# The first layer of a graph network on one core: one ScalarE sum for the ranks of two edge tiles, widened blocks for both halves, one set of rows per group

## The chip, the cores and the metric

The kernel runs on one core of a Trainium2 chip. The time is device time of one execution in microseconds (us), and the median over runs is compared. The engines go by their short names: PE multiplies matrices (PEld is its loading of weights), DVE is VectorE, ACT is ScalarE, POOL is GpSimd, and SP is SyncE, which here issues most DMAs. Each engine works off its own list of instructions in order and waits on semaphores for the others.

## What is computed

There are N = 12500 nodes with 256 features and E = 200000 edges, sorted by their target `dst`. Two layers follow each other. The change touches the first one only:

```python
# L0: x (N,256) -> 4 heads of 32 columns, for "self" (order 0) and "neighbour" (order 1)
feat = relu(einsum('nd,ohdk->ohnk', x, W) + b)
att_s = leaky(einsum('hnk,hk->hn', feat[0], a_self))
att_n = leaky(einsum('hnk,hk->hn', feat[1], a_neigh))
edge_w = (att_s[:, src] + att_n[:, dst]) * edge_weight
agg = segment_sum(edge_w[..., None] * feat[1][:, dst, :], src, N)     # by src, which is not sorted
feat = stack([feat[0], agg]); feat = normalised over each head, scaled, shifted
x = layernorm(x + concat(feat))
# L1: messages relu([x[src], x[dst]] @ W_msg + b_msg), summed by dst; update, two layernorms
```

## The kernel before

The program has three stages on one time axis.

**Stage one** (`with ExitStack() as l0`) cuts the edges into 112 groups (`NG`) of 14 tiles (`GT`) of 128 edges. Since `dst` is sorted, a group's targets lie in a window of 128 rows of x, whose first row is read into a register (`base_reg`). For each group two things are made.

- *Features* (`feat_tasks`): `load_group` fetches the window's rows `xw` for the neighbour half and, for the first 98 groups (`NB` blocks of 128 rows), also the aligned row block `xb` for the self half. `transposes` and `keep` turn both, `project` multiplies them with the weights, `relu`, `att_mult`, `att_sum`, `mean_sum` and `centre` make centred features `F` and attention scores. `part0` to `part3` split the neighbour half into three bf16 parts `F3`. The self half goes to DRAM (`out_f`, to `selfd`), its scores stay in SBUF (`atts`, by `leaky_s`).
- *A counting sort by source block* (`sort_tasks`): the 14 tiles' edges are put in order of their source's block of 128 nodes. `widen` (ACT) spreads the block numbers of the first seven tiles over 99 columns. `hot` compares these with a ramp, `hot_b` compares the other seven tiles' block numbers, broadcast, with the ramp; both make the one-hots `A`. `pair`, `ranks`, `quarter`, `rows`, `begins`, `keep_v` give, for each edge's partition and each block, the rank `V` at which an edge of that block goes. `place_mm` (PE) puts `V + BIG * A` in PSUM for each tile, in chunks of 5, 5 and 4 tiles. `place_pick` (ACT, 14 times a group) takes relu of that minus `BIG` and sums it over the columns: one rank for each edge of a tile. `split` (DVE) splits the ranks in row and column numbers, `hot_r`, `goods`, `hot_q` (DVE) and `permute` (PE) move the edges' data to their places, `rel_keep`, `rel_turn`, `rel_row`, `rel_out`, `rel_in` bring the target rows over DRAM to all partitions, and `hot_n` makes one-hots `oT` of them. `message` (PE) multiplies these with `F3`, `evict` (ACT) copies the products to SBUF, and four `scatter`s (POOL, indirect DMAs) write them to a log in DRAM, in which each source block has its own stretch. `extras` writes the edges' source and weight beside the messages.

Every eighth group a chunk of edge data (`meta_load`, `meta_tasks`: names `m_...`) is prepared for the next eight.

The order is written out by hand: the table `AT` gives each task of group g a place `256 * g + AT[name]`, and all tasks of all groups are sorted by it. PE, ACT, DVE and SP each issue their tasks in that order (`manual_schedule`, which names these four engines and not POOL). A place modulo 256 tells what lies beside what: 256 units are one group.

**Stage two** (`with ExitStack() as bar`) goes through the 98 source blocks: `log_load` fetches a block's log, `log_hot` and `log_sum` sum it with one-hot matmuls, `heads_a` to `heads_d` combine the two sums with the self scores and normalise, `own_s` to `own_d` do the same for the self half `fs`, which `load_y` fetches from `selfd`, and `stats` to `store_x1` make the rows for layer two. **Stage three** (`with ExitStack() as l1`) goes through the edges again, 14 tiles a group, gathers source rows (L1346) and sums messages.

Of the kernel before, what the change touches and what calls it, by code (L numbers as in the profile page):

```python
# [11 lines left out]
def _warn_once_fixed(msg, *args, **kwargs):  # L12
# [28 lines left out]
    "widen": -453, "hot": -365, "hot_b": -265, "pair": -179, "ranks": -86, "quarter": -64, "rows": -29,  # L41
    "begins": 13, "keep_begins": 55, "keep_v": 51, "shift": 161, "reach": 262, "steps": 227, "steps_keep": 243,
    "steps_low": 256, "target": 313, "index": 400, "place_mm0": 52, "place_mm1": 63, "place_mm2": 204,
    "pick0": 73, "pick1": 78, "pick2": 78, "pick3": 87, "pick4": 123, "pick5": 144, "pick6": 156, "pick7": 170,
    "pick8": 179, "pick9": 219, "pick10": 229, "pick11": 239, "pick12": 249, "pick13": 280, "split": 339,
    "hot_r": 358, "goods": 374, "hot_q": 371, "permute": 424, "rel_keep": 435, "extras": 477, "rel_turn": 502,
    "rel_row": 552, "rel_out": 574, "rel_in": 595, "hot_n": 959, "message0": 997, "evict0": 1053,
    "message1": 1032, "evict1": 1063, "message2": 1056, "evict2": 1082, "message3": 1065, "evict3": 1121,
    "message4": 1101, "evict4": 1165, "message5": 1188, "evict5": 1203, "scatter0": 1120, "scatter1": 1146,
    "scatter2": 1197, "scatter3": 1206, "load": -331, "transposes": 47, "keep": 68, "project": 80, "relu": 295,  # L50
    "att_mult": 355, "mean_sum": 459, "att_sum": 438, "centre": 467, "leaky_n": 498, "part0": 584, "part1": 636,
    "part2": 665, "part3": 705, "leaky_s": 585, "out_f": 634, "m_load": -1689, "m_cast0": -1234,
    "m_cast1": -1433, "m_col0": -1201, "m_keep0": -1125, "m_col1": -698, "m_keep1": -614, "m_col2": -941,
    "m_keep2": -861, "m_block": -1073, "m_place": -877, "m_high": -378, "m_rest": -285, "m_mid": 263,
    "m_low": 351, "m_win": -76, "m_turn": -866, "m_pairs": -710, "m_mask": -535, "m_count": 210,
}
BIG = 4096.0
# [43 lines left out]
def kernel(  # L101
# [45 lines left out]
    selfd = dram.tile([ROWS, HD], FT, name="selfd")  # L147
# [12 lines left out]
    atts = consts.tile([P, NB, H], FT, name="atts")  # L160
# [55 lines left out]
    with ExitStack() as l0:  # L216
# [28 lines left out]
        nc.vector.memset(nbig, -BIG)  # L245
        quart = dcp.tile([P, 1], FT, name="quart")
# [178 lines left out]
        xb = {}  # L425
        F3 = {}

        def load_group(g):
            if g < NG:
                b = base_reg(g) if g else 0  # L430
                xw[g] = xin.tile([P, D], FT, name="xw")
                nc.sync.dma_start(xw[g], x[bass.ds(b, P), :])
            if g < NB:
                xb[g] = xin.tile([P, D], FT, name="xb")
                n = min(P, N - g * P)
                if n < P:
                    nc.vector.memset(xb[g], 0.0)
                nc.sync.dma_start(xb[g][:n], x[g * P:g * P + n, :])

        def feat_tasks(g):  # L440

            ww, bb = g < NG, g < NB
            o0, o1 = (0 if bb else 1), (2 if ww else 1)
            lo, hi = o0 * HD, o1 * HD
            st = {}

            def flat(t):
                return t[:, lo:hi]

            def heads(t):  # L450
                return t[:, lo:hi].rearrange("p (a k) -> p a k", k=32)

            def transposes():
                tp = ps.tile([P, 512], FT, name="tp", bufs=1)
                if ww:
                    for c in range(2):
                        nc.tensor.transpose(tp[:, c * P:(c + 1) * P], xw[g][:, c * P:(c + 1) * P], ident)
                if bb:
                    for c in range(2):
                        nc.tensor.transpose(tp[:, (2 + c) * P:(3 + c) * P], xb[g][:, c * P:(c + 1) * P], ident)  # L460
                st["tp"] = tp

            def keep():
                xT = feat.tile([P, 4, P], FT, name="xT")
                a, z = (0 if ww else 2), (4 if bb else 2)
                nc.scalar.copy(xT[:, a:z].rearrange("p c q -> p (c q)"), st["tp"][:, a * P:z * P])
                st["xT"] = xT

            def project():
                fp = bank[g][:, 0:D] if ww else ps.tile([P, 512], FT, name="fs")[:, 0:D]  # L470
                nc.tensor.matmul(fp[:, lo:hi], ones3, bias3[:, lo:hi], start=True, stop=False)
                for o in range(o0, o1):
                    for c in range(2):
                        nc.tensor.matmul(
                            fp[:, o * HD:(o + 1) * HD], st["xT"][:, (2 + c) if o == 0 else c, :],
                            w0s[:, c, o * 4:(o + 1) * 4, :].rearrange("p a k -> p (a k)"),
                            start=False, stop=(o == o1 - 1 and c == 1))
                st["fp"] = fp
# [69 lines left out]
        def sort_tasks(g):  # L548
# [97 lines left out]
            def place_pick(t):  # L646
                def f():
                    i, k = divmod(t, 5)
                    if t == 0:
                        small("sl", GT, p=P)  # L650
# [1040 lines left out]
```

## Time and profile before

| what | value |
|---|---|
| median of 10 runs | 4406.07 us (4403.0 to 4410.87) |
| profiled execution: time, span | 4406.86 us, 4405.1 us |
| stage one: first scatter starts, last scatter starts | 53.5 us, 1079.1 us |
| stage two: first and last matmul of L972 start | 1088.6 us, 1999.6 us |
| stage three: first and last matmul of L1424 start | 2027.3 us, 4390.0 us |
| granted PE clock, whole span | 0.924 |

The span is what the profiled instructions cover; the time of that execution is 1.8 us longer and lies within the ten runs. The page cuts the span in 40 slices of 110 us and gives the busy share of each in tenths, 9 for 90% or more:

```profile
PE   8999999997999999997777777777777777777776
...
DVE  9999999996999999995545555555555555555555
ACT  8999999996122222224444444444444444444444
POOL 2555555555666666664666666666666666666664
PEclk9999999998999999998888889889889898888888
```

The first ten slices are stage one, the next eight stage two, the rest stage three. In other views a line reads: source line, engine, operation, output<-inputs by the program's names, shapes; then either count, busy time, mean duration and idle time before, or (in a timeline) start and duration first. Where the engine stood idle before an instruction, a timeline line ends with the idle time and what ended it in brackets.

### The profile page before, as it was taken

Reading aid. Unit: us, or ns where it says so; the run is one execution under the profiler, and the core shown is the slowest. Engines: PE = TensorE matmul, PEld = TensorE weight load, DVE = VectorE, ACT = ScalarE, POOL = GpSimd, SP = SyncE. Lnnn points to the kernel's source line nnn. Section 1 sums busy time; section 2 is a strip of 40 time slices with the busy share of each in tenths; the row PEclk is TensorE's granted clock in tenths of the full one; section 3 lists DMA queues with packets and bytes.
Section 4 is the critical chain, followed back from the end, with each engine's and each line's share of the span. In section 5 each row is a group of like instructions: output and inputs, shape, how many; then the busy total and the mean of one; then the engine's idle time right before and its main releaser. Section 6 shows DMA issues by size and latency. Waiting matters only on the chain. (4 is left out here: it accounts for less than half of the span.)

```text
span 4405.1 us, 82564 instructions
## 1 busy us (share of the span) xinstructions
PE 3701.0 (84%) x24976; PEld 3130.7 (71%) x24976; DVE 3164.1 (72%) x9205; ACT 2374.0 (54%) x8379; POOL 2667.8 (61%) x2542
## 2 busy tenths in 40 slices
PE   8999999997999999997777777777777777777776
PEld 6888888876888888885666666656665666666665
DVE  9999999996999999995545555555555555555555
ACT  8999999996122222224444444444444444444444
POOL 2555555555666666664666666666666666666664
PEclk9999999998999999998888889889889898888888
DMA  5887766666666666664555555555555555555554
GB/s 193 278 270 264 247 216 217 218 202 212 180 192 191 190 192 190 192 187 127 145 144 144 140 145 143 140 143 143 146 139 146 140 144 144 147 141 142 141 144 113
DMA packets 470159, 763.55 MB, mean 173 GB/s; under 512 B 76202, under 2 KB 313504, under 8 KB 469712
## 3 DMA queue, kind: packets, MB, share of 16 engines
q1 hardware_dynamic: 339552, 415.13, 33.2%
q0 software_dynamic: 110848, 327.87, 24.2%
q10 hardware_dynamic: 19312, 15.21, 1.1%
q8 instruction: 204, 3.34, 0.3%
q14 instruction: 243, 1.99, 0.2%
HBM read 559.81 MB, written 198.12 MB: 172 GB/s over the span
## 5 line engine op out<-in xcount | busy, mean ns | idle before, releaser
L1346 POOL DMA_INDIRECT gb<-pd,srcf x1563 | 1501.7, 961 | 881.5 <-issue 483.2
L1424 PE MATMUL agg<-gb,o 128*128 128x256 f32 x3126 | 940.4, 429 | 309.7 <-ACT gb L1407 183.5
L1405 DVE TENSOR_TENSOR gb<-qp,gb 128x512 f32<-128x512 f32 x781 | 531.7, 681 | 768.7 <-remote 206.2
L1424 PEld LDWEIGHTS agg<-gb,o 128*128 128x128 f32 x3126 | 645.6, 215 | 485.6 <-ACT gb L1407 233.0
L731 POOL DMA_INDIRECT log<-m,ix x448 | 550.6, 1229 | 527.3 <-ACT m L725 148.3
L972 PE MATMUL sum<-lg,o 128*128 128x256 f32 x3724 | 839.3, 379 | 15.3 <-DMA lg<-log 13.7
L1407 ACT ACTIVATE gb<-gb 128x512 f32<-128x512 f32 x781 | 486.7, 626 | 645.6 <-DVE gb L1405 443.8
L972 PEld LDWEIGHTS sum<-lg,o 128*128 128x128 f32 x3724 | 696.0, 189 | 115.8 <-POOL lg L959 13.8
L964 DVE TENSOR_SCALAR o<-iotap,lg 128x128 f32<-128x128 f32 x1862 | 612.9, 399 | 38.9 <-PE sum L972 31.0
L651 ACT ACTIVATE junk<-wp,nbig 128x99 bf16<-128x99 f32 x1568 | 602.2, 457 | 1.2 <-PE wp L624 0.7
L1383 PE MATMUL qp<-qh,oT 128*128 128x256 f32 x1563 | 596.9, 401 | 4.4 <-DVE rs L1253 1.6
L959 POOL TENSOR_TENSOR lg<-lg 128x512 f32<-128x512 f32 x392 | 431.7, 1114 | 224.8 <-DMA lg<-log 161.8
L651 ACT ACTIVATION_READ_ACCUMULATOR junk<-wp,nbig 128x1 f32 x1568 | 472.2, 314 | 0.0
L1383 PE MATMUL qp<-ql,oT 128*128 128x256 f32 x1563 | 440.7, 301 | 0.0
L718 PE MATMUL mp<-F,oT 128*128 128x132 bf16 x5376 | 418.2, 222 | 21.7 <-ACT m L725 8.5
L718 PEld LDWEIGHTS <-oT 128*128 128x128 bf16 x5376 | 343.3, 99 | 53.5 <-issue 19.2
L1391 ACT ACTIVATE o<-iotac,rel 128x128 f32<-128x128 f32 x782 | 267.8, 391 | 180.0 <-PE agg L1424 76.1
L725 ACT COPY m<-mp 128x396 f32<-128x396 f32 (+1 forms) x672 | 349.7, 565 | 16.2 <-PE mp L718 11.0
L1383 PEld LDWEIGHTS qp<-qh,oT 128*128 128x128 f32 x1563 | 331.5, 212 | 31.7 <-PE agg L1424 4.3
L1383 PEld LDWEIGHTS qp<-ql,oT 128*128 128x128 f32 x1563 | 331.0, 212 | 24.6
L1387 DVE TENSOR_TENSOR o<-iotac,rel 128x256 f32<-128x256 f32 x390 | 161.3, 414 | 241.5 <-remote 55.7
L890 PE MATMUL qm<-wms,xT 128*128 128x256 f32 x224 | 97.9, 527 | 273.0 <-ACT xT L885 193.6
(263 smaller groups left out, 6566.3 us busy)
## 6 DMA issues: line engine op xcount, KB each, us to landing
lg<-log SPq DMA_DIRECT2D x392, 268.0 KB
dr<-in_dst_dram SPq DMA_DIRECT2D x781, 128.0 KB
rr<-reld SPq DMA_DIRECT2D x112, 512.0 KB
log<-zero SPq DMA_DIRECT2D x101, 268.0 KB
gb<-pd,srcf POOLq DMA_INDIRECT x1563
lg<-log SPq DMA_DIRECT2D x98, 201.0 KB
xw<-in_x_dram SPq DMA_DIRECT2D x112, 128.0 KB
xw<-x1d SPq DMA_DIRECT2D x112, 128.0 KB
```

Of the source, the lines that this page charges most:

```text
L651: nc.scalar.activation(small("junk", NBX, BF, p=P), st["w", i][:, k * NBE:k * NBE + NBX], AF.Relu, bias=nbig, accum_out=st["sl"][:, t:t + 1])
L718: nc.tensor.matmul(mp[:, r * (HD + H):(r + 1) * (HD + H)], st["oT"][:, r0 + r], F3[g][:, k], start=(k == 0), stop=(k == 2))
L725: nc.scalar.copy(st["m"][:, r0:r0 + n, 0:HD + H], st.pop(("mp", i))[:, :n * (HD + H)].rearrange("p (r w) -> p r w", r=n))
L731: ins = nc.gpsimd.indirect_dma_start(out=log[:, :], out_offset=bass.IndirectOffsetOnAxis(ap=st["ix"][:, k:k + 1], axis=0), in_=st["m"][:, ...
L959: e.tensor_tensor(t[:, 1, :n, 0:HD].rearrange("p r (h k) -> p r h k", h=H), t[:, 0, :n, 0:HD].rearrange("p r (h k) -> p r h k", h=H), t[:, ...
L964: nc.vector.tensor_scalar(o[:, r], iotap, t[:, 0, r, MW - 2:MW - 1], t[:, 0, r, MW - 1:MW], op0=OP.is_equal, op1=OP.mult)
L972: nc.tensor.matmul(sums[b], o[:, r], t[:, :, r, 0:HD], start=(k == 0 and r == 0), stop=(k == NK - 1 and r == n - 1))
L1346: nc.gpsimd.indirect_dma_start(out=gb[s][:r, i], out_offset=None, in_=pd[:, :], in_offset=bass.IndirectOffsetOnAxis(ap=srci[:r, t:t + 1], ...
L1383: nc.tensor.matmul(qp[:r, i], oT[:, i * P:i * P + r], q, start=(k == 0), stop=(k == 1))
L1405: nc.vector.tensor_tensor(z, qp, z, op=OP.add)
L1407: nc.scalar.activation(z, z, AF.Relu)
L1424: nc.tensor.matmul(agg[g], o[:r, i], z[:r, i], start=(j == 0 and i == 0), stop=lastmm)
```

## The change

1. *Ranks of two tiles in one sum.* `BIG` becomes 2^23. `keep_w` (ACT) writes a second copy of `V` times `PACK` = 2048 beside it; `place_mm` uses `V` for even tiles and `2048 * V` for odd ones, in chunks of 4, 4, 4 and 2 tiles. `place_pick` runs seven times on two tiles' columns: the sum is the even tile's rank plus 2048 times the odd tile's. `unpack` (ACT) and `apart` (three small operations on POOL) take the two apart: the odd rank by rounding, the even one as the rest. `split` then reads the same 14 ranks as before.
2. *`widen` spreads all 14 tiles*, and `hot_b` compares widened blocks as `hot` does.
3. *Both halves of the features from the window's rows.* `xb` and its load, transposes and copies are gone; `project` makes 256 columns from `xw` in two matmuls. The self half is written to `selfd` at the window's rows, by a register's address, with the four self scores beside it (132 columns); windows overlap, and the rows that two of them share are written twice, with the same values. `atts` is gone: stage two reads the scores with `fs`, whose tile gets a third buffer. All 112 groups do the full work of both halves.
4. *`src_keep`*: the copy of the source column in `extras` goes from DVE to ACT.
5. *A new order*: nearly every entry of `AT` changes. The work put between named tasks at the start is kept in its order by `due`.

```diff
 AT = {
-    "widen": -453, "hot": -365, "hot_b": -265, "pair": -179, "ranks": -86, "quarter": -64, "rows": -29,
-    "begins": 13, "keep_begins": 55, "keep_v": 51, "shift": 161, "reach": 262, "steps": 227, "steps_keep": 243,
-    "steps_low": 256, "target": 313, "index": 400, "place_mm0": 52, "place_mm1": 63, "place_mm2": 204,
...
-    "rel_row": 552, "rel_out": 574, "rel_in": 595, "hot_n": 959, "message0": 997, "evict0": 1053,
...
-    "part2": 665, "part3": 705, "leaky_s": 585, "out_f": 634, "m_load": -1689, "m_cast0": -1234,
...
+    "widen": -485, "hot": -379, "hot_b": -361, "pair": -303, "ranks": -160, "quarter": -124, "rows": -119,
+    "begins": -64, "keep_begins": -22, "keep_v": -3, "shift": 31, "reach": 165, "steps": 131, "steps_keep": 205,
+    "steps_low": 259, "target": 261, "index": 333, "keep_w": -3, "place_mm0": 5, "place_mm1": 43,
+    "place_mm2": 64, "place_mm3": 165, "pick0": 43, "pick1": 50, "pick2": 111, "pick3": 147, "pick4": 149,
+    "pick5": 195, "pick6": 196, "unpack": 205, "apart": 281, "split": 290, "hot_r": 309, "goods": 359,
+    "hot_q": 357, "permute": 428, "rel_keep": 461, "extras": 529, "src_keep": 542, "rel_turn": 465,
+    "rel_row": 513, "rel_out": 555, "rel_in": 560, "hot_n": 818, "message0": 922, "evict0": 944,
...
+    "scatter2": 1124, "scatter3": 1153, "load": -402, "transposes": -250, "keep": -167, "project": 2,
+    "relu": 167, "att_mult": 184, "mean_sum": 517, "att_sum": 470, "centre": 546, "leaky_n": 607, "part0": 630,
+    "part1": 673, "part2": 741, "part3": 804, "leaky_s": 640, "out_f": 1160, "m_load": -1865, "m_cast0": -1677,
...
-BIG = 4096.0
+BIG = 2.0 ** 23
+PACK = 2048.0
...
-    selfd = dram.tile([ROWS, HD], FT, name="selfd")
+    selfd = dram.tile([ROWS, H + HD], FT, name="selfd")
...
         def load_group(g):
-            if g < NG:
-                b = base_reg(g) if g else 0
-                xw[g] = xin.tile([P, D], FT, name="xw")
-                nc.sync.dma_start(xw[g], x[bass.ds(b, P), :])
-            if g < NB:
-                xb[g] = xin.tile([P, D], FT, name="xb")
-                n = min(P, N - g * P)
-                if n < P:
-                    nc.vector.memset(xb[g], 0.0)
-                nc.sync.dma_start(xb[g][:n], x[g * P:g * P + n, :])
+            xreg[g] = base_reg(g) if g else 0
+            xw[g] = xin.tile([P, D], FT, name="xw")
+            nc.sync.dma_start(xw[g], x[bass.ds(xreg[g], P), :])
...
+                nc.tensor.matmul(fp, ones3, bias3, start=True, stop=False)
+                for c in range(2):
+                    nc.tensor.matmul(fp, st["xT"][:, c, :], w0s[:, c].rearrange("p a k -> p (a k)"),
+                                     start=False, stop=(c == 1))
...
             def out_f():
-                nc.sync.dma_start(selfd[g * P:(g + 1) * P, :], st["F"][:, 0:HD])
+                nc.sync.dma_start(selfd[bass.ds(xreg[g], P), :], st["F"][:, 0:H + HD])
...
-            CH = [(0, 5), (5, 5), (10, 4)]
+            CH = [(a, min(4, GT - a)) for a in range(0, GT, 4)]
...
             def widen():
-                st["bx"] = srt.tile([P, h, NBX], BF, name="bx")
-                nc.scalar.copy(st["bx"], blk[c][:, j * GT:j * GT + h, None].to_broadcast([P, h, NBX]))
+                st["bx"] = srt.tile([P, GT, NBX], BF, name="bx")
+                nc.scalar.copy(st["bx"], blk[c][:, tl, None].to_broadcast([P, GT, NBX]))
...
             def hot_b():
-                b = blk[c][:, j * GT + h:j * GT + GT, None].to_broadcast([P, h, NBX])
-                nc.vector.tensor_tensor(st["A"][:, h:], iotab[:, h:], b, op=OP.is_equal)
+                nc.vector.tensor_tensor(st["A"][:, h:], iotab[:, h:], st["bx"][:, h:], op=OP.is_equal)
...
             def keep_v():
-                nc.scalar.copy(small("v", NBE, FR, p=P), st["V"])
+                nc.scalar.copy(small("v", 2 * NBE, FR, p=P)[:, :NBE], st["V"])
+
+            def keep_w():
+                nc.scalar.activation(st["v"][:, NBE:], st["V"], AF.Copy, scale=PACK)
...
-                    nc.tensor.matmul(o, identr, st["v"][:, None, :].to_broadcast([P, n, NBE]),
+                    nc.tensor.matmul(wp[:, :n * NBE].rearrange("p (t b) -> p t b", b=2 * NBE), identr,
+                                     st["v"][:, None, :].to_broadcast([P, n // 2, 2 * NBE]),
                                      start=True, stop=False)
...
-                    nc.scalar.activation(small("junk", NBX, BF, p=P), st["w", i][:, k * NBE:k * NBE + NBX], AF.Relu,
-                                         bias=nbig, accum_out=st["sl"][:, t:t + 1])
+                    i, t = k // 2, 2 * k % 4
+                    if k == 0:
+                        small("s7", h, p=P)
+                    nc.scalar.activation(
+                        small("junk", 2 * NBX, BF, p=P).rearrange("p (t b) -> p t b", b=NBX),
+                        st["w", i][:, t * NBE:(t + 2) * NBE].rearrange("p (t b) -> p t b", b=NBE)[:, :, :NBX],
+                        AF.Relu, bias=nbig, accum_out=st["s7"][:, k:k + 1])
...
+            def unpack():
+                nc.scalar.activation(small("t7", h, p=P), st["s7"], AF.Identity, bias=nhalf, scale=1.0 / PACK)
+
+            def apart():
+                sl = small("sl", GT, p=P)
+                odd = sl.rearrange("p (k w) -> p k w", w=2)[:, :, 1]
+                nc.gpsimd.tensor_scalar(odd, st["t7"], MAGIC, -MAGIC, op0=OP.add, op1=OP.add)
+                even = sl.rearrange("p (k w) -> p k w", w=2)[:, :, 0]
+                nc.gpsimd.tensor_single_scalar(even, odd, PACK, op=OP.mult)
+                nc.gpsimd.tensor_tensor(even, st["s7"], even, op=OP.subtract)
...
             def extras():
                 m = st["m"] = msgp.tile([P, NR, MW], FT, name="m")
-                nc.vector.tensor_copy(m[:, :, MW - 2], st["go"][:, :, 1])
                 nc.vector.tensor_reduce(m[:, :, MW - 1], st["go"][:, :, 2:5], AX.X, OP.add)
+
+            def src_keep():
+                nc.scalar.copy(st["m"][:, :, MW - 2], st["go"][:, :, 1])
...
-        for g in range(max(NG, NB)):
+        for g in range(NG):
...
-                                    atts[:, b:b + n, :, None].to_broadcast([P, n, H, 32]), op=OP.mult)
+                                    fs.pop(q)[:, :n, 0:H, None].to_broadcast([P, n, H, 32]), op=OP.mult)
...
-            fs[q] = bw.tile([P, BB, HD], FT, name="fs")
+            f = fs[q] = bw.tile([P, BB, H + HD], FT, name="fs", bufs=3)
```

## The prediction

> **What bounds the kernel.** I read the busy time by stretches first, because the share of the span mixes three stages.
>
> ```profile
> core 0: us, PE busy (x) PEld busy (x) DVE busy (x) ACT busy (x) POOL busy (x), PEclk, DMA share, GB/s
> ...
> 300.00:500.00 200.00, 191.35 (x2343) 162.70 (x2342) 191.94 (x606) 196.86 (x980) 108.37 (x85) 0.99 0.79 266
> ...
> 1400.00:1600.00 200.00, 200.00 (x950) 174.10 (x949) 191.73 (x533) 47.33 (x111) 137.35 (x115) 1.00 0.65 189
> ```
>
> In the first stage (to about 1084 us) PE, DVE and ACT are all above 95%: nobody waits long, and no single share names the bound. The second stage (first sum matmul at 1088.6, last at 1999.6) is PE at 200.00 of 200, and the third (from 2027) runs the gathers; the change alters only operands there. So everything is decided by the pace of the 112 groups of stage one. The source view of the multiply of `goods`, once per group, gives that pace:
>
> ```profile
> L669 DVE TENSOR_TENSOR mv<-rh,em x85: 1310/1318/1323, 104.0 to 884.0; 128x1120 bf16<-128x1120 bf16 x85
> ...
> L669 DVE TENSOR_TENSOR mv<-rh,em x11: 1312/1318/1319, 958.1 to 1045.7; 128x1120 bf16<-128x1120 bf16 x11
> ```
>
> 84 steps in 780.0 us are 9.29 us per group; the last groups, which have no second row block, take 87.6/10 = 8.76.
>
> Which engine sets 9.29? The durations of neighbours overlap, so I take from the timeline, for every shape, the median time from its start to the next start on its engine, times its count, between 200 and 900 us (75 groups). That gives DVE 9.18 us per group, ACT 8.97, PE 8.42. DVE is the bound with 0.11 us lost, ACT stands 0.2 us behind it. The timeline of DVE, with start and duration in its first columns:
>
> ```profile
> 701.68 0.51 DVE L568 TENSOR_TENSOR A<-iotab,bx 128x693 bf16<-128x693 bf16 x1
> 702.11 0.21 DVE L609 SCALAR_TENSOR_TENSOR dl<-pos,capc,begun 99x1 f32<-99x1 f32 x1
> ...
> 704.42 0.18 DVE L697 COPY m<-mp 128x16 f32<-128x16 f32 x1
> 704.50 0.20 DVE L698 TENSOR_REDUCE m<-mp 128x16 f32<-128x48 f32 x1
> ...
> 704.75 0.87 DVE L572 TENSOR_TENSOR A<-iotab,blk 128x693 bf16<-128x693 bf16 x1
> 705.54 0.15 DVE L635 TENSOR_TENSOR dw<-fs,dh 99x1 bf16<-99x1 f32 x1
> ```
>
> Start to start, the half of the one-hot that reads ACT's widened blocks (L568) costs 0.43 us, the half that reads the broadcast itself (L572) 0.79, the copy L697 0.08. No line has an idle time in brackets. And ACT:
>
> ```profile
> 400.23 0.35 ACT L651 ACTIVATE junk<-wp,nbig 128x99 bf16<-128x99 f32 x1
> 400.45 0.22 ACT L651 ACTIVATION_READ_ACCUMULATOR junk<-wp,nbig 128x1 f32 x1
> 400.55 0.36 ACT L651 ACTIVATE junk<-wp,nbig 128x99 bf16<-128x99 f32 x1
> ...
> 705.91 0.52 ACT L482 ACTIVATE R<-fs 128x256 f32<-128x256 f32 x1
> 706.18 0.25 ACT L693 CAST rT<-tp 16x128 bf16<-16x128 f32 x1
> ...
> 706.89 0.83 ACT L564 COPY bx<-blk 128x693 bf16<-128x693 bf16 x1
> 707.56 0.64 ACT L466 COPY xT<-tp 128x512 f32<-128x512 f32 x1
> 708.04 0.37 ACT L514 CAST F<-F 128x132 bf16<-128x132 f32 x1
> ```
>
> One pick with its read of the sum is 0.32 us, 256 columns 0.27, the widening 0.67, 512 columns 0.48.
>
> **The change, part by part (us per group).** *DVE:* `hot_b` reads widened blocks like `hot`: 0.79 to 0.43, -0.36. The copy in `extras` goes to ACT: -0.08. The attention, centring and part operations keep their sizes. DVE: 9.18 - 0.44 = 8.74.
>
> *ACT:* 14 picks at 0.319 are 4.47. Seven of 198 columns: no row has that form. Bounds are 0.32 (width free) and 0.545 (two picks, one read of 0.093 saved). Copies of 132 and 396 columns at 0.148 and 0.369 give 0.84 ns a column, so 0.319 + 99 x 0.84 ns = 0.40, and I take that: 2.81, -1.66. Widening 1386 instead of 693 columns: between 0.67 and 1.34; by the same slope 1.25, +0.58. `keep` of 256 columns instead of 512: -0.20. `keep_w`, as `keep_v` (0.133): +0.13. `unpack`, as the small L587 (0.144): +0.14. `src_keep`, as L686 (0.063): +0.06. Sum -0.95: ACT 8.02. With both upper bounds it is 9.11, still under 9.29.
>
> *PE:* two transposes fewer at 0.07 to 0.11: -0.14 to -0.22. The projection is four matmul instructions of 256 columns instead of eight of 128: 8 x 0.112 = 0.90, against 4 x 0.245 (911.0 us over 3724 of that shape in stage two) = 0.98, +0.08. The place matmuls have the same columns in four chunks instead of three: 2 x (0.316+0.222) + 0.270 + 0.180 = 1.53, against 3 x 0.45 + 0.28 (200 columns on the line through 400 and 500) = 1.63, +0.10. PE stays at 8.4.
>
> *POOL* gets `apart`, three operations on 128x7, where it had only the scatters:
>
> ```profile
> L959 POOL TENSOR_TENSOR lg<-lg 128x512 f32<-128x512 f32 x392 | 431.7, 1114 | 224.8 <-DMA lg<-log 161.8 <-PE sum L972 51.0 <-PE qm L1060 3.9
> ...
> L1122 POOL TENSOR_TENSOR fs<-fs,scb 128x128 f32<-128x128 f32 x3 | 1.4, 455 | 13.4 <-ACT v L1007 13.1 <-DVE fs L1112 0.3
> ```
>
> Between 0.16 (the IOTA of one column) and 0.455 each; the line through these rows gives 0.25 at 7 columns, 0.74 for the three. POOL has 424.6 busy us of 789.5, so there is room. It matters only through the new wait: `split` on DVE now waits for POOL, and behind it are `centre`, `hot_n`, the one-hots and so all of PE's messages. I follow the new order, 256 units to a group: `goods` at 103, then ACT's `rel_keep` (behind PE's `permute`, 0.84), `steps_keep`, `unpack` at 205, `apart` at 25 of the next, `split` at 34. From the end of `goods` to `split` DVE has 3.6 us of work (one-hots 0.86, `pair` 0.43, `reach` 0.39, two reductions 0.77, `att_mult` 0.34, the rest small); the other way is 1.1 + 0.25 + 0.74 and some 0.3 for semaphores, 2.4. Slack 1.2 us, if POOL is free. So `apart` costs nothing, hidden behind those 3.6 us; without that cover it is 0.74 to 1.4.
>
> *DMAs and SP:* the xb load goes (one issue of 0.4 us and 128 KB). `out_f` moves from 634 to 1160, behind `rel_out`, `rel_in` and loads of two later groups, with an address from a register, so each write may wait for the one before, a group earlier and long landed; F has four buffers and is centred again only 410 units later. `rel_in` to `hot_n` shrinks from 364 to 258 units. The packets of that load end 4.1 us after its issue in the median, 6.7 at most, and it is issued 2.1 us after `rel_out` (5.6 is SP's longest wait there): 6.2, at worst some 12, against 305 units = 10.6 us. Free, but for rare groups. The xw load comes 152 units before its transposes; its packets end after 2.9 us (3.5 at most), against 5.3. In stage two the scores come with `fs` instead of from `atts`; PE sets the pace there: nothing, and at worst 3 us once, for the first `fs` that waits for the last `out_f`.
>
> **The sum.** DVE 8.74 plus today's loss of 0.11 is 8.85. Of DVE's 9.18, 0.69 is the next metadata, which comes in some groups only (8.49 without it); in the others DVE now has 8.05 and PE's 8.4 leads; I add half of 0.35 in three of eight groups, 0.06: 8.90 (8.75 with no friction, 9.05 with twice the loss). 98 groups x (8.90 - 9.29) = -38. The last 14 had no second block and now do the full work: 13 x 0.14 = +2. Head and tail: as before. The profiled execution took 4406.9 (span 4405.1), the median is 4406.1: 4406.9 - 36 = **4370.5**, own range 4354 to 4387.
>
> **A rule against the change.** A scatter that lies beside `hot_q` and `goods` on DVE lasts 3.31 us, one that doesn't 0.96 (next fence). The Trainium skill, GPSIMD Engine Reference, speaks against `apart` on POOL twice: its section "4.1 Engine selection" puts elementwise work on VectorE, and its section "1. Specifications" says that POOL's way to SBUF is shared with DVE instructions that read two SBUF inputs or use both ports. By that page each of the three operations could wait out a DVE operation of some 0.4 us, 1.2 in all, which is just the slack worked out above; the sum would still be 4370, but with nothing left over.
>
> **Rivals.** *POOL holds up `split`* (slower):
>
> ```profile
> 707.83 3.31 POOL L731 DMA_INDIRECT log<-m,ix  x1 [0.30 <-ACT bx L564]
> 711.45 1.73 POOL L731 DMA_INDIRECT log<-m,ix  x1 [0.30 <-ACT F L518]
> ...
> 715.44 0.96 POOL L731 DMA_INDIRECT log<-m,ix  x1 [0.35 <-ACT rT L693]
> ```
>
> A scatter that starts with `hot_q` (707.79) lasts through it and `goods`: 3.31. If the new phase puts one there in every group with two more behind it, `apart` ends 3.61 + 2 x 1.26 + 0.74 = 6.9 us after the start of `hot_q`, while DVE reaches `split` after 1.00 + 1.24 + 3.6 = 5.8: 1.0 us late, each group: 4370 + 112 = 4483. From 0.33 us late it is slower than before. For it: a third engine between ACT and DVE, and POOL's order isn't the list's. Against: only 9 of 299 scatters took over 2.9 us, and POOL is idle 46%.
> *Half is given back* by ACT (its upper bounds, 9.11) or by stalls at pairs that now stand close, `quarter` to `rows` 5 units, `keep_w` to `place_mm0` 8, `steps_low` to `target` 2: a period of 9.12, 98 x -0.17 + 13 x 0.36 = -12, 4395.
> *It does not do what it says:* the loss between the engines grows by what is saved, or the stage's end is set by the tail, 4406.
>
> **Chances.** The forecast 0.58, half given back 0.17, no change 0.07, POOL 0.18. A measurement here tells 0.2% (9 us) from none; the forecast and most of the second case lie beyond it: faster 0.74, same 0.08, slower 0.18. The range reaches down to a period with no friction and up past "no change", 4352 to 4415; POOL's case is left out.
>
> **What would show it.** Right: `goods` comes every 8.9 us, L651 seven times per group at about 0.40 start to start, the second one-hot 0.43, and no bracket before `split`. Wrong: idle time before `sl` on DVE, released by POOL; `goods` every 9.3 or more; DVE waits before `oT` for its load.

## The result, and the profile after

| kernel | median | against before, 95% interval | profiled execution: time, span |
|---|---|---|---|
| before, beside it | 4407.65 us (28 runs) | 1 | 4406.86, 4405.1 |
| changed | 4428.86 us (4425.25 to 4437.07, 8 runs) | 1.0050 (1.0042 to 1.0059) | 4432.07, 4430.2 |

The change made the kernel slower by 0.5%, 21 us, where 36 us less were forecast. Its page, busy tenths in 40 slices of 110.8 us:

```profile
PE   8999999997999999997777777777777777777776
...
DVE  8999999997999999995555555555555555555555
ACT  7889989887122222223444444444444444444444
POOL 3556556656766666664666666666666666666664
PEclk8999999999999999998888888898888889888889
```

ACT, at 9 throughout stage one before, now has slices of 7 and 8, and POOL has risen by the three new operations. DVE still shows nines, though it has less to do. The stretch that was shown of before, and the view of `goods` (the multiply), in the changed kernel:

```profile
300.00:500.00 200.00, 184.67 (x2232) 157.02 (x2232) 184.21 (x570) 178.18 (x727) 120.45 (x147) 0.98 0.75 250
```

```profile
L660 DVE TENSOR_TENSOR mv<-rh,em x112: 1307/1314/1367, 29.1 to 1079.9; 128x1120 bf16<-128x1120 bf16 x112
```

Columns of the first: busy us of PE, PEld, DVE, ACT and POOL with their instructions, then PE's clock, DMA share and GB/s. No engine is above 93% any more; before, three stood at 96 to 98%. From the first to the last `goods` the changed kernel takes 1050.8 us, before took 1024.4: **the pace of a group went from 9.23 to 9.47 us** (111 steps). Those 26.4 us are a little more than the whole difference of the two spans, 25.1. The way from there to stage two is 3.6 us shorter, stage two 1.7 shorter, stage three 4.2 longer.

Where did the saved work go? For each line and shape I take the shortest usual time from its start to the next start on its engine (the 3rd of 100), which leaves waits out, and call the rest of the time idle. Per group, between 200 and 900 us:

```
                   DVE work  idle    ACT work  idle    pace there
before               8.98    0.34      8.91    0.41      9.32
changed              8.51    0.98      8.17    1.33      9.49
```

The work fell, by 0.47 on DVE as forecast, and by 0.74 on ACT, 0.2 less than forecast. Idle time took its place, on both engines. Who ended it, in the view of waits from 100 to 1000 us (engine and line, what it waited for: us in total, times, longest; waits of POOL and of PE's weight loads are left out):

```profile
...
ACT m L718 <- PE mp L711: 29.9, 60, 1.0
PE fs L453 <- ACT v L583: 27.2, 75, 1.2
...
ACT junk L629 <- PE wp L602: 17.9, 41, 1.8
...
DVE dl L586 <- ACT begun L577: 8.8, 31, 1.0
DVE sl L649 <- POOL sl L644: 8.3, 8, 1.4
...
DVE rows L565 <- ACT rows L561: 7.3, 12, 1.3
```

PE's projection waits for ACT's `keep_w` (L583; both work on the PSUM tile `bank[g]`, on different columns), ACT's evictions and picks wait for PE, and DVE for both. `split` (L649) waits for POOL eight times only.

### The profile page after: what moved, and what is told of

It is laid out like the page before. It is cut to its first block, busy times and chain, and to the rows that moved or that the text cites. A ratio compares the mean times of both kernels' runs of the same rounds, so it can differ in the third digit from the quotient of the medians.

```text
span 4430.2 us, 81215 instructions
## 1 busy us (share of the span) xinstructions
PE 3690.9 (83%) x24612; PEld 3121.8 (70%) x24612; DVE 3144.3 (71%) x9108; ACT 2304.0 (52%) x7147; POOL 2763.3 (62%) x2878
## 5 line engine op out<-in xcount | busy, mean ns | idle before, releaser
L711 PE MATMUL mp<-F,oT 128*128 128x132 bf16 x5376 | 391.7, 222 | 8.1 <-issue 5.0
L629 ACT ACTIVATE junk<-wp,nbig 128x198 bf16<-128x198 f32 x784 | 341.8, 458 | 52.9 <-PE wp L602 31.2
L718 ACT COPY m<-mp 128x396 f32<-128x396 f32 (+1 forms) x672 | 303.0, 465 | 63.7 <-PE mp L711 40.7
L1371 DVE TENSOR_SCALAR oT<-dr,baseP 128x256 fp32r<-128x256 int32 x782 | 282.5, 361 | 11.0 <-issue 11.0
```

The lines of the kernel that those rows point to most:

```text
L629: nc.scalar.activation(small("junk", 2 * NBX, BF, p=P).rearrange("p (t b) -> p t b", b=NBX), st["w", i][:, t * NBE:(t + 2) * NBE].rearrang ...
L711: nc.tensor.matmul(mp[:, r * (HD + H):(r + 1) * (HD + H)], st["oT"][:, r0 + r], F3[g][:, k], start=(k == 0), stop=(k == 2))
L718: nc.scalar.copy(st["m"][:, r0:r0 + n, 0:HD + H], st.pop(("mp", i))[:, :n * (HD + H)].rearrange("p (r w) -> p r w", r=n))
```

## The experiments

They ran on several chips. "Pace" is first to last `goods` over 111; "late" is explained below, with what it can't tell. Each ratio is against the kernel before on the same chip.

| label | ratio (95%) | pace | late | before there |
|---|---|---|---|---|
| before, with the verdict | | 9.229 | 479 of 1658 | 4407.65 |
| changed, with the verdict | 1.0050 (1.0042 to 1.0059) | 9.466 | 430 of 1783 | 4407.65 |
| e1_old_order | 1.0164 (1.0148 to 1.0181) | 9.750 | 2 of 1536 | 4009.32 |
| e2_project_later | 0.9989 (0.9979 to 0.9999) | 9.115 | 12 of 1714 | 4009.32 |
| e3_apart_dve | 0.9998 (0.9989 to 1.0008) | 9.198 | 15 of 1805 | 4009.32 |
| e4_widen_alone | 1.0134 (1.0118 to 1.0151) | 9.675 | 46 of 1600 | 4009.32 |
| c_after (changed) | 0.9949 (0.9935 to 0.9963) | 8.993 | 10 of 1848 | 4008.76 |
| e5_three_covers | 0.9979 (0.9970 to 0.9988) | 9.086 | 13 of 1725 | 4008.76 |
| e6_apart_twice | 1.0046 (1.0031 to 1.0060) | 9.356 | 18 of 1796 | 4008.76 |
| e7_both | 1.0025 (1.0016 to 1.0034) | 9.315 | 15 of 1695 | 4008.76 |
| b_before (before) | one run, 4007.43 us | 9.171 | 24 of 1662 | 4010.25 |
| c_after_again (changed) | 0.9944 (0.9927 to 0.9960) | 8.974 | 10 of 1853 | 4010.25 |
| e8_project_again | 0.9986 (0.9977 to 0.9996) | 9.190 | 13 of 1698 | 4010.25 |
| e9_evict_later | 0.9967 (0.9953 to 0.9981) | 9.073 | 7 of 1834 | 4010.25 |
| c_after_third (changed) | 1.0040 (1.0026 to 1.0054) | 9.348 | 384 of 1796 | 4376.87 |
| e10_before_held | 1.0034 (1.0023 to 1.0045) | 9.345 | 455 of 1649 | 4376.87 |
| e11_after_held | 1.0188 (1.0168 to 1.0208) | 10.008 | 276 of 1688 | 4376.87 |
| e12_later_held | 1.0128 (1.0111 to 1.0145) | 9.714 | 364 of 1634 | 4376.87 |
| e13_later_again | 1.0118 (1.0101 to 1.0135) | 9.604 | 439 of 1652 | 4404.77 |
| e14_wide_pairs | 1.0071 (1.0054 to 1.0088) | 9.627 | 311 of 1649 | 4404.77 |

Chips came in two kinds: before takes 4009 to 4010 us on one and 4377 to 4408 on the other. Most of that gap lies in stage three, which the change hardly touches (first to last of its sums: 1973 to 1978 us against 2331 to 2367). There the granted PE clock differs too, 0.99 against 0.87 to 0.88; in stage one it is 0.96 to 1.00 in the traces of both kinds.

### One part at a time

**e4_widen_alone**: the kernel before, and only the widening of all blocks.

```diff
-nc.scalar.copy(st["bx"], blk[c][:, j * GT:j * GT + h, None].to_broadcast([P, h, NBX]))
+nc.scalar.copy(st["bx"], blk[c][:, tl, None].to_broadcast([P, GT, NBX]))
...
-nc.vector.tensor_tensor(st["A"][:, h:], iotab[:, h:], b, op=OP.is_equal)
+nc.vector.tensor_tensor(st["A"][:, h:], iotab[:, h:], st["bx"][:, h:], op=OP.is_equal)
```

> The kernel before with one part of the change alone: ACT widens all 14 tiles and hot_b compares widened blocks. By the forecast's own sums DVE falls from 9.18 to 8.82 us per group and ACT rises from 8.97 to 9.55, so ACT becomes the bound: 9.6 to 9.7 per group, 4440 to 4455. If DVE alone set the pace of before, it would get faster instead: 4370 to 4385.

The stretch from 300 to 500 us of this run:

```profile
300.00:500.00 200.00, 185.82 (x2258) 156.01 (x2259) 183.42 (x581) 200.00 (x933) 97.75 (x83) 1.00 0.76 257
```

ACT is at 200.00 of 200. Its work is 9.50 us a group (8.91 before, so +0.59 where +0.58 was forecast) and DVE's 8.63 (-0.35, forecast -0.36). The pace is 9.675, as expected: ACT has become the bound. The time rose by 54 us, a little more than the 34 to 49 expected. The terms of the sum hold, and the widening pays only with the picks' saving.

**e1_old_order**: the changed kernel in the order of before, the new tasks put in.

```diff
-"widen": -485, ... "keep_w": -3, ... "unpack": 205, "apart": 281, "split": 290, ...
+"widen": -453, ... "keep_w": 52, ... "unpack": 251, "apart": 285, "split": 339, ...
```

> The changed kernel with the order of before: every task that both kernels have goes back to its old place in AT, and the new tasks are put beside the old ones that they stand for (keep_w after keep_v, pick0 to pick6 where the old 14 picks lay, unpack and apart between the last pick and split). Theory ORDER (the work per group fell as forecast, but the new order sets up waits between PE and ACT that give it back): stage one goes from 9.47 us per group to between 8.9 and 9.1, the time to 4365 to 4392. Rival POOL (the three small operations on POOL and the wait of split on them cost the time): they are still there, so 4420 or more. Rival WORK (the new forms themselves cost more than the old): 4420 or more.

DVE's timeline, the lines with idle time:

```profile
640.83 0.18 DVE L649 SCALAR_TENSOR_TENSOR sl<-sl,twin 128x14 f32<-128x14 f32 x1 [0.80 <-POOL sl L644]
651.46 0.18 DVE L649 SCALAR_TENSOR_TENSOR sl<-sl,twin 128x14 f32<-128x14 f32 x1 [0.79 <-POOL sl L644]
```

Here the rival about POOL is real: `split` waits 0.8 us for `apart`. In the old order `unpack` follows too late. It isn't the only wait: from 100 to 1000 us, ACT's new `src_keep` (L691), put right behind `extras` (L688), waits for that as long.

```profile
ACT m L691 <- DVE m L688: 75.1, 88, 1.8
DVE sl L649 <- POOL sl L644: 65.6, 92, 0.8
```

The theory that the old order would win the time back (8.9 to 9.1 us a group) missed. The old order with these places for the new tasks is no way out; the new one hides `apart`.

**e3_apart_dve**: `apart` on DVE.

```diff
-nc.gpsimd.tensor_scalar(odd, st["t7"], MAGIC, -MAGIC, op0=OP.add, op1=OP.add)
+nc.vector.tensor_scalar(odd, st["t7"], MAGIC, -MAGIC, op0=OP.add, op1=OP.add)
```

(and the other two alike)

> The changed kernel with the three operations of apart on DVE instead of POOL, everything else and the order as in the changed kernel. Rival POOL: the wait for POOL goes (0.11 us per group in front of split, and what scatters lose), 4405 to 4418. Theory ORDER: DVE takes on three operations of some 0.1 to 0.2 us and loses the short wait, so the same or slower, 4428 to 4470.

DVE's work is 8.99 again and its idle time 0.18; the pace is 9.198. The changed kernel on chips of the same kind runs at 8.97 to 8.99: the three operations are better on POOL, by 0.2 us.

### The close pairs, moved apart

**e2_project_later**: `"project": 2` becomes 41 and `"place_mm0": 5` becomes 20.

> The changed kernel with two places of the new order altered: project from 2 to 41 and place_mm0 from 5 to 20, so that PE has target, the transposes and one message to do while ACT makes keep_v and keep_w. Theory ORDER: the wait of 0.51 us per group that PE shows in front of project mostly goes, stage one falls by 0.15 to 0.4 us per group, the time to 4385 to 4412. Rivals POOL and WORK: 4425 to 4433, as the changed kernel.

**e5_three_covers**: e2, with `"rows": -119` at -104 and five buffers for `ix` instead of four.

> As e2_project_later (project at 41, place_mm0 at 20), and two more waits of DVE covered: rows goes from -119 to -104, behind hot_b, so that DVE has the second one-hot to do while ACT makes quarter, and ix gets a fifth buffer, so that index does not wait for an old scatter. Theory RING (PE, ACT and DVE wait for each other once around per group; each gap that is covered shortens the round until DVE's own 8.5 us of work is reached): e2's waits in front of rows (0.13) and ix (0.14) go, 8.85 to 9.05 us per group, 12 to 35 us below the kernel before. If e2 had already taken all there is (the waits only move to the next place): 9.1 to 9.2, within 0.2% of the kernel before.

**e7_both**: e2 and e3 together.

> project at 41 and place_mm0 at 20 as in e2, and apart on DVE as in e3, together. Theory RING: with apart DVE has 8.9 us of work and shows only 0.17 of waiting in e3, so the second cover finds nothing more to give: 9.05 to 9.2 us per group, within 0.2% of e3. If the two were separate losses that add up (0.35 and 0.28 of 9.47): 8.8 to 8.9, 35 us or more below the kernel before.

**e6_apart_twice**: e3, and POOL makes the same three operations again into tiles that nobody reads.

> As e3_apart_dve (apart on DVE), and POOL does the same three operations too, into tiles that nobody reads: only the hop through POOL is out of the chain, POOL's work and its way to SBUF are as in the changed kernel. Theory RING (the hop from ACT over POOL to DVE is what e3 saved): 9.15 to 9.25 us per group, as e3, within 0.2% of the kernel before. Rival PORT (POOL's three operations, and the scatters that they shift beside hot_n, slow DVE down): back to 9.35 to 9.5, 12 to 26 us above the kernel before.

**c_after**: the changed kernel, unchanged, beside e5 to e7.

> The changed kernel as it is, on the chip of the other runs of this call, as their base. Stage one at 9.4 to 9.5 us per group from the first goods to the last, as in its first profile; 20 to 26 us above the kernel before, whatever the chip's clock in stage three.

The last was meant as a measure and turned the study: **the same program is 0.5% faster than before here.** Nothing that was moved beats it: e2 and e5 are 0.003 to 0.004 slower than it, e7 0.008. e5 and e7 came out slower than their theory of the ring had it (9.09 and 9.32 against at most 9.05 and 9.2); e5 lies by its rival, that the waits only move to the next place (9.1 to 9.2). By e6 against e3 the unread POOL work costs 0.16 us a group, though nobody waits for it by name, as the rival about the port had it; by which way it costs that was not looked into. So pulling the close pairs apart gains nothing on this kind of chip, and the question became what differs between the chips.

### What differs: when a finished matmul is known

The changed kernel's ACT and PE around the evictions of two message chunks, first with the verdict (start, duration, engine, line; in brackets the idle time before and who ended it):

```profile
698.65 1.21 PE L711 MATMUL mp<-F,oT 128*128 128x132 bf16 x18
...
699.41 0.20 ACT L629 ACTIVATION_READ_ACCUMULATOR junk<-wp,nbig 128x1 f32 x1
699.66 0.43 PE L599 MATMUL wp<-v,identr 128*128 128x400 f32 x1
...
700.49 0.88 ACT L718 COPY m<-mp 128x396 f32<-128x396 f32 x2 [0.88 <-PE mp L711]
```

and in c_after_again:

```profile
662.59 1.21 PE L711 MATMUL mp<-F,oT 128*128 128x132 bf16 x18
...
663.36 0.20 ACT L629 ACTIVATION_READ_ACCUMULATOR junk<-wp,nbig 128x1 f32 x1
663.45 0.88 ACT L718 COPY m<-mp 128x396 f32<-128x396 f32 x2
663.61 0.43 PE L599 MATMUL wp<-v,identr 128*128 128x400 f32 x1
```

PE does the same at the same distance: 18 messages, then a place matmul 1.01 and 1.02 us after their start. The first eviction needs nine of the 18. In c_after_again it starts 0.86 us after the first message, with no idle time. With the verdict ACT is done with its pick at 699.61 and starts 1.84 us after the first message, at 700.49: it learns late of matmuls that, by PE's own records, were long done. The trace's records of PE's signals say the same: one at 698.90 us, the next only at 700.47, and three more by 700.67, though matmuls that signal had started at 699.12, 699.64, 699.94 and 700.24. The signals come late and in a bunch. Two records of PE's signals within 60 ns stand in stage one 25 times in before and 102 times in the changed kernel with the verdict, and never in any trace of the other kind.

To count this, I took every matmul from 30 to 1080 us that signals and the time from its start to PE's next recorded signal (0.1 us later at least). The usual value is 0.23 to 0.36 us, depending on the matmul; "late" in the table means over 0.6 us. It is 24 to 29% on the chip of the verdict **for both kernels** and 0.1 to 3% on the other kind. This count tells the kinds apart, but it is no measure of the delay, because on the late kind records of signals are also missing: there are 1384 for the 1658 matmuls of before that signal, and 1564 for 1783 in the changed kernel (b_before 1638 for 1662, c_after_again 1846 for 1853). ACT's and DVE's signals lack records there as well, about a fifth to a quarter, and yet a projection that waited for `keep_w` started 0.05 us after its end, in the median, in both kinds. So the delay is better read from those who wait. An eviction can start 0.255 us after its chunk's last matmul at the earliest, in every trace. Those before which ACT stood idle for over 50 ns, of 672:

```
                          that waited   start after the chunk's     of the wait, later than 0.255 us
                                        last matmul, median         after that matmul, per group
before, with the verdict       20              0.66 us                      0.11 us
changed, with the verdict     111              0.96                         0.54
b_before                        8              0.34                         0.00
c_after_again                  45              0.26                         0.00
c_after_third                 113              0.90                         0.49
```

Before rarely read a result so early that it had to wait. The changed order does so in 99 of 112 groups. The delay at the evictions alone, about half a microsecond a group, is about as large as what the changed kernel's pace differs between the kinds (9.47 and 9.35 against 8.97 to 8.99). Nothing else in stage one was found to differ: the granted clock is alike, and the work per group, as above, is 8.98 and 8.96 on DVE and 8.91 on ACT for before and b_before, and 8.51 on DVE and 8.17 and 8.20 on ACT for the changed kernel and c_after_again.

**b_before, c_after_again, e8_project_again (e2 again), e9_evict_later** (`evict3`, 4, 5 at 1130, 1140, 1165; scatters 25 units later), on one chip:

> The kernel before, unchanged, for its trace on this chip. Theory LATE: the chips differ in how late a finished matmul tells the other engines. On the chip of the verdict 479 of 1658 of PE's signals in stage one came over 0.6 us after their matmul's start in the kernel before, and 430 of 1783 in the changed one; on the two other chips about 10. The old order reads PE's results long after they are made, so this kernel's pace hardly depends on it: 9.1 to 9.25 us a group on any chip, 20 waiting evictions or fewer. Theory RHYTHM (the same program falls into one of two steady rhythms by its first groups, whatever the signals do): the same pace, no link to the signals.

> The changed kernel, unchanged, a third time. LATE: if few of PE's signals are late here (under 3%), the pace is 8.95 to 9.05 and the ratio 0.993 to 0.997, and waiting evictions start 0.26 us after their last matmul; if a quarter is late, the pace is 9.4 to 9.5 and the ratio 1.003 to 1.007, and they start 0.9 us after it. RHYTHM: either pace, with few late signals too.

> The changed kernel with project at 41 instead of 2 and place_mm0 at 20 instead of 5 (as e2_project_later), now beside the changed kernel on one chip. LATE: on a chip with few late signals it is not needed and costs a little, 0.997 to 1.000 of the kernel before and 0.003 to 0.004 above the changed kernel; on a chip with many it takes the close step from keep_w to project out of the ring and is faster than the changed kernel by 0.003 or more. RHYTHM: no order between the two can be told.

> The changed kernel with the evictions 3, 4 and 5 some 0.4 us later in ACT's list (1130, 1140, 1165) and the scatters 25 units later. LATE: on a chip with many late signals the evictions' waits (0.62 us a group there) fall by half or more and the pace by 0.1 to 0.3; on a chip with few, within 0.2% of the changed kernel, or slower by up to 0.4% if PE then waits for a message buffer. RHYTHM: same as the changed kernel, or a jump by the whole 0.4 us.

With few late signals the pace falls from 9.171 to 8.974. The waits of c_after_again, from 100 to 1000 us:

```profile
ACT junk L629 <- PE wp L602: 23.4, 87, 0.3
...
PE fs L453 <- ACT v L583: 14.8, 58, 0.5
...
ACT m L718 <- PE mp L711: 9.4, 10, 1.7
```

The projection still waits for `keep_w`, half as long, and no wait of DVE for ACT or POOL is among the 20 largest. From the 56th to the 96th group this kernel runs at 8.82 us against 9.20 for b_before: -0.38, where -0.39 was forecast. In the first half (groups 8 to 56) it is 9.15 against 9.31; there DVE waits 0.2 us a group at `ix` (L622) for scatters of earlier groups. e8 and e9 came out as the theory of late signals had it for such a chip: cover that is not needed costs 0.4 and 0.2%. The rival RHYTHM, by which the same program falls into either pace whatever the signals do, did not show: the changed kernel's four traces have the slow pace where signals are late and the fast one where they aren't.

### PE held on purpose

That late signals go with the loss doesn't show that they make it. So PE was held in both kernels, by seven bias matmuls whose result is overwritten:

```diff
             def project():
                 ...
+                for _ in range(7):
+                    nc.tensor.matmul(fp, ones3, bias3, start=True, stop=True)
                 nc.tensor.matmul(fp, ones3, bias3, start=True, stop=False)
```

(`fp[:, lo:hi]` in the kernel before). They take 0.79 us of PE a group (0.75 in the kernel before).

**c_after_third**, the changed kernel:

> The changed kernel, unchanged, a fourth time, as the measure of the next three. LATE: with few late signals from PE (under 3% over 0.6 us) pace 8.95 to 9.05 and 0.993 to 0.997; with a quarter of them late 9.4 to 9.5 and 1.003 to 1.007. RHYTHM: either, whatever the signals.

**e10_before_held:**

> The kernel before with seven more bias matmuls in each projection, whose result is overwritten: PE is held there for 7 x 0.11 = 0.8 us a group (up to 1.4, if one takes 0.195), as the late signals hold its readers. PE has 7.4 us of work a group, so it has the room. LATE: the old order reads late, so the pace rises by 0.15 at most, ratio 1.000 to 1.005. Rival WORK (any 0.8 us more on PE costs each order the same): before and after rise alike.

**e11_after_held:**

> The changed kernel with the same seven matmuls. LATE: the ring from keep_w over the projection and the messages to the eviction and back to keep_w has 0 to 0.3 us of room at a pace of 8.97, so of 0.8 us some 0.5 to 0.8 shows: pace 9.4 to 9.8, ratio 1.004 to 1.016, and ACT waits for PE before the evictions and before the picks and DVE for ACT, as on the chip of the verdict. WORK: as much as the kernel before rises. RHYTHM: the hold only moves phases, so the pace stays at 9.0 or goes to 9.4, not beyond.

**e12_later_held** (`project` at 41, `place_mm0` at 20, and held):

> The changed kernel with project at 41 and place_mm0 at 20 and the same seven matmuls. LATE: the close step from keep_w to project is out of the ring, so less of the hold shows than in e11: pace 9.2 to 9.5, ratio 0.999 to 1.008 and below e11. WORK: 9.2 plus what before rises.

This chip was of the kind with late signals, and the changed kernel was slower again, 1.0040. The same 0.8 us of PE cost the old order 0.11 us a group (13 us of medians over 112 groups) and the new one 0.61 (68 us; 0.66 by the paces). The rival by which any work on PE costs both orders the same is out. e11's total lies above its range because that was made from a pace of 8.97, and the hold came on top of 9.348. e12 lies below e11, as expected, but above its own range. Its base is the same order without the hold, and that is slow itself where signals are late: e13, below, has 9.604. Against that the hold costs 0.11 us a group in e12 (on another chip of the kind), against 0.66 in e11: with the projection moved away from `keep_w`, hardly more of it shows than in the old order. PE was not held on a chip with punctual signals, so how much room the ring has there is not measured. The waits of e11, from 100 to 1000 us:

```profile
ACT junk L631 <- PE wp L604: 70.7, 51, 2.8
ACT junk L631 <- PE tp L445: 55.8, 38, 1.7
...
PE fs L454 <- ACT v L585: 24.0, 75, 0.6
DVE ix L624 <- PE fs L620: 21.0, 61, 1.4
DVE rows L567 <- ACT rows L563: 20.0, 29, 2.3
```

and the largest one of ACT for PE in e10:

```profile
ACT xT L466 <- PE fs L642: 8.8, 12, 1.1
```

**e13_later_again** (e2 a third time) and **e14_wide_pairs** (e13 with `rows` at -104, the evictions and scatters of e9, five buffers for `ix`), to learn by which pair it enters:

> The changed kernel with project at 41 and place_mm0 at 20, as in e2_project_later. LATE: where a quarter of PE's signals is late, the step from keep_w to project no longer carries them round, so the ratio is below the changed kernel's 1.004 to 1.005: 0.997 to 1.002; where few are late 0.998 to 1.000 as twice before. If it is 1.004 or more with late signals, the ring closes over another pair and this pair alone is not the place.

> e13 with three more pairs pulled apart: rows at -104, the evictions 3 to 5 some 0.4 us later in ACT's list with the scatters 25 units later, and a fifth buffer for ix. LATE: with late signals the lowest of all orders of the changed kernel, 0.995 to 1.001; with few 0.997 to 1.001, since each move also delays work that had no wait.

Both missed: with late signals they are slower than before, by 1.2 and 0.7%, and no better than the changed order. In e13 the projection no longer waits for `keep_w`, but now the transposes (L445) wait for ACT's `rT` (L684) and DVE's `rows` for ACT, 0.2 and 0.3 us a group:

```profile
DVE rows L565 <- ACT rows L561: 24.6, 34, 1.4
...
PEld tp L445 <- ACT rT L684: 20.9, 61, 0.8
```

In e14 the evictions hardly wait (21 instead of 111), and the picks wait for PE instead, 1.0 us a group:

```profile
ACT junk L629 <- PE wp L602: 47.8, 63, 2.5
ACT junk L629 <- PE mp L711: 39.8, 36, 1.8
```

Taking one pair apart sends the wait to the next. That the round trip between PE and ACT is too long as a whole, and not one pair of it, is how I read this; no run shows it by itself. An order that beats both kernels where signals are late was not found; where they aren't, the changed kernel was the fastest of all that ran.

## Why the prediction was wrong

- **The terms of work were right where it mattered.** DVE -0.44 forecast, -0.47 measured. A pick of two tiles with its read took 0.31 + 0.09 (0.40 forecast), the widening 1.25 (1.25), `apart` 0.28, 0.26 and 0.20 (0.25 each). ACT fell by 0.74 instead of 0.95: `unpack` took 0.20 (0.14) and `src_keep` 0.14 to 0.2 (0.06). That error was harmless, ACT's 8.17 being below DVE's 8.51.
- **The step that failed** is "DVE 8.74 plus today's loss of 0.11 is 8.85". The loss between the engines was carried over from the old order. Measured the same way in both kernels it went from 0.34 to 0.98 with the verdict and, as the other chips show, from 0.29 to 0.45 with punctual signals. 8.51 + 0.98 is the pace from 200 to 900 us; 8.51 + 0.45 = 8.96 would nearly have been the forecast of 8.90, and there the change gains 0.5 to 0.6% where 0.8% was forecast.
- **What stood in its place.** Follow the chain back from `goods`, start by start between 300 and 950 us, and step to the releaser wherever an engine stood idle over 40 ns: in the changed kernel, with the verdict, a period of 9.49 us consists of 4.9 to 5.0 us of ACT, 3.7 to 4.0 of PE with its signals, and 0.4 to 0.9 of hops between engines, depending on where a hop is taken to begin. DVE is hardly in it (0.06). In before DVE has 6.3 to 7.1 of 9.31, in c_after_again 5.5 to 6.4 of 8.94. The ring is `keep_w`, projection, messages, evictions, picks, the next `keep_w`. Where signals are punctual it closes within DVE's time, where they are late it sets the pace, and of 0.8 us by which PE is held 0.6 to 0.66 show in it (e11). The prediction followed one way, from `goods` over POOL to `split`, found 1.2 us of slack, which held with the new order, and never closed the way from ACT back to PE.
- **The rivals.** POOL at `split` did not come (8 waits of it in 900 us); it came in the old order (e1). "Half is given back by stalls at close pairs" had the right kind of cause and the wrong size: 9.12 against 9.47 with the verdict. Of its three pairs `quarter` to `rows` shows (DVE `rows`); the pairs that cost most, `keep_w` to the projection and message to eviction, weren't named. The start of the new order leaves 5 units, 0.18 us, between `keep_w` and the projection, and even the punctual hop takes 0.32.
- **Could it have been read?** In part: in before's own trace the 20 evictions that waited started 0.66 us after their last matmul in the median, where 0.255 is possible. It was not asked how long after a matmul its reader learned of it, because nearly nobody waited.

## What to carry to other kernels

Shortening an engine's work and tightening the order are two changes: price the second by closing every ring between engines, with the signal times that the trace shows at those who wait, including the late ones. A loss between engines belongs to an order and can't be carried to another. Where a verdict is half a per cent, run the unchanged kernel on a second chip before explaining it: here the sign depends on that.

## What the runs showed of the hardware

- **Signals of PE come late on some chips.** There, in stage one, evictions that waited for PE started 0.90 and 0.96 us after their last matmul in the changed kernel, where 0.26 us is usual elsewhere, and PE's signals have records within 60 ns of each other, 96 and 102 times against none. Matmuls' recorded starts don't change (messages 0.06 us apart in both), and the granted clock of stage one doesn't tell it: in before, with the verdict, it was 1.00 from 53 to 340 and from 364 to 1050 us, and so it was in b_before. ACT's signals were not seen to reach PE late: the projections that waited for `keep_w` started 0.05 us after its end, in the median, in both kinds. It isn't settled whether it belongs to the chip or to the time: one chip number showed both kinds, with 4009 and with 4377 us for before. What makes the signals late stays open too. The Trainium skill, "TensorE: Matmul & The Clock Gate", section "The cost: per-tile semaphore tail", has the increments of a semaphore by several matmuls queue for some 26 ns each. By that figure the four signals of the bunch above would need about 0.1 us, an estimate from that page; the first of them came 1.36 us after its matmul's start, so this doesn't explain it.
- **Traces of that kind lack records.** In stage one 12 to 17% of PE's signals have no record of their own in before and the changed kernel, elsewhere up to 3%. A long time to the next record is then not yet a late signal; when the reader starts is.
- **POOL beside DVE.** In c_after_again, POOL's timeline:

```profile
650.72 0.86 POOL L641 TENSOR_SCALAR sl<-t 128x7 f32<-128x7 f32 x1 [0.80 <-ACT t L636]
659.36 0.30 POOL L641 TENSOR_SCALAR sl<-t 128x7 f32<-128x7 f32 x1 [1.36 <-ACT t L636]
```

The same operation on 7 columns takes 0.3 or 0.86 us. Beside the two-input `pair` of DVE its median in this run is 0.78 (63 times), beside a reduction 0.28 (27 times). The rule that the prediction weighed, that POOL waits out such instructions, fits what is seen here, mainly for the first of the three operations; it stayed within the slack.
